# Two graph layers run group by group, or the first layer for all groups and then the second with one wide right matrix

## The chip, the core and the metric

The kernel runs on one core of a Trainium2 chip. Such a core has a matrix engine (PE; its weight loads are listed apart as PEld), a vector engine (DVE), a scalar engine (ACT), a third elementwise engine (POOL) and a queue (SP) that here does nothing but issue transfers. PE writes its sums to eight banks of PSUM, each 512 float32 wide on 128 partitions; DVE and ACT read and write PSUM and SBUF, POOL works on SBUF alone. The metric is the time of one execution on the device, in microseconds (us).

## The reference

There are 128 graphs of 128 nodes with 512 features each. Two layers follow one another, each with a residual and a layer norm.

```python
# layer 0: x (128, 128, 512), adj (128, 128, 128), W (512, 1024)
deg = sum(adj, -1)
agg = einsum('bij,bjf->bif', adj, x) / maximum(deg, 1e-6)
x = layernorm(x + relu(concat([x, agg], 2) @ W.T))

# layer 1: Wv (512, 512), Wk (3, 512, 512)
Xw = x @ Wv + bv
sj, si = Xw @ aw[:512, 0], Xw @ aw[512:, 0]
e = leaky_relu(sj[:, None, :] + si[:, :, None] + ab[0], 0.2)
alpha = adj * exp(e)
T = alpha / (sum(alpha, -1) + 1e-12)
H, Xk = 0, x
for k in range(3):
    H, Xk = H + Xk @ Wk[k] + bk[k], einsum('bij,bjd->bid', T, Xk)
x = layernorm(x + relu(H))
```

All of it is float32. Since T acts on the left and the weights on the right, H is x Wk0 + T (x Wk1 + T (x Wk2)) plus the biases. Likewise agg W' is A (x W') with A the row-scaled adjacency. So each layer is one large product of x with weights, and then small products with a 128 x 128 matrix for each graph. Both kernels work in this order. The scores sj and si are products of x with two vectors of 512.

## The kernel before

**Groups and streams.** Four graphs make a group; there are 32 groups. For each group two sequences of PE work are written out as Python generators. `stream0` (line 287) is the first layer of the group, 18 steps long (`NA`, line 671). `stream1` (line 563) is the second layer of two graphs, so it runs twice for a group. The main loop (lines 769 to 776) takes one step of the first and one step of the second in turn; the second lags 24 steps (`LAG`), so it works on the group before. Everything else, the loads, turns, sums, norms and scores, is a function that is put at a numbered half step by three tables (`EARLY`, `PLACES`, `LATE`, lines 685 to 721). Each engine carries out its instructions in exactly the order in which the Python code emits them.

**Fast products.** The large products are made by the seven-product scheme (Strassen in Winograd's form): both operands are cut into 2 x 2 blocks, sums of blocks are formed, and seven block products take the place of eight. In the first layer two levels are used: the operand is 512 rows (four graphs) by 512, the right one 512 x 512 (twice, for x and for agg), so there are 49 products of 128 x 128 by 128 x 256. `outer_pair` (line 256) makes two outer products at once, the two halves of a bank; its products are called `prod(bank, k)`. `x_turn`, `x_inner` and `x_s1` to `x_s4` (lines 214 to 233) turn x and form its left sums. In the second layer one level is used for each two graphs: seven products by [Wk2 Wk1], each of two matmuls with 512 columns, and seven by Wk0, each of two with 256 columns, with `left_sums` formed by `y_sums` (line 247). `wk_sums` (line 657) forms the right sums once.

**How one outer product runs.** The products accumulate in four banks, called X, Y, W and Z. The first product goes to X; ACT copies X to Y, a second goes to Z and ACT copies it to s5; a third is added to X, and DVE forms W = X + s5; one product is added to Y, which is then done; a further one is added to X and DVE forms Z = X + s5; one product is added to W, and the last to X. So a product into X has to wait until an addition has read X. All matmuls come from line 251, in `mm`.

**Between the layers.** `residual` (DVE) takes relu, adds x and sums the row; `y_stats`, `y_scales` and `y_norm` (ACT and POOL) make the norm. `y_scores` (line 446) takes the two dots of the unnormalized y with `wrow` on DVE, eight for a group. y is stored to memory (`y_store`) and loaded again in 32-row blocks (`y_load`), which together with a DVE transpose inside 32 x 32 blocks turns it. T takes the same road: `t_scores` stores the scores (`scd`), `t_load` loads them on all partitions, `t_exp` (ACT) makes leaky relu and exp, `t_sums` (DVE) multiplies by the adjacency and sums, `t_norm` scales, and T goes to memory (`sd`) and back (`Tb`) to be turned. The y tiles have four buffers (`py`).

Of the kernel before, what the change touches and what calls it, by code (L numbers as in the profile page):

```python
# [16 lines left out]
def kernel(  # L17
# [14 lines left out]

# [5 lines left out]
    H = NC // 2  # L61
    FH = F // 2
    G = 4
    NG = B // G
    assert N == P and F == 512 and wk.shape[2] == F and K == 3 and B % G == 0
    DEG_EPS, ROW_EPS, LN_EPS, SLOPE = 1e-6, 1e-12, 1e-5, 0.2

# [3 lines left out]
    py = ctx.enter_context(tc.tile_pool(name="py", bufs=4))  # L71
    dram = ctx.enter_context(tc.tile_pool(name="dram", bufs=3, space=bass.MemoryType.DRAM))
    small = ctx.enter_context(tc.tile_pool(name="small", bufs=4))
    psum = ctx.enter_context(tc.tile_pool(name="psum", bufs=1, space=bass.MemoryType.PSUM))


    R = 32
    Q = P // R
    xbs, adjs, ys = {}, {}, {}

    def load_blocks(dst, src):

        M = src.shape[2] // Q
        for q in range(Q):
            nc.sync.dma_start(dst[q * R : (q + 1) * R].rearrange("r b j m -> r (b j) m"),  # L85
                              src[:, :, q * M : (q + 1) * M].rearrange("b (j r) m -> r (b j) m", r=R))

    def load_x(g, p):

        b = g * G + 2 * p  # L90
        ys[g, p] = py.tile([P, 2, F], FP, name="y")
        nc.sync.dma_start(ys[g, p], x[b : b + 2].rearrange("b n f -> n b f"))

    def load_x_blocks(g, p):
        b = g * G + 2 * p
        xbs[g, p] = p2.tile([P, 2, Q, P], FP, name="xb", tag="xb")
        load_blocks(xbs[g, p], x[b : b + 2])

    def load_adj(g):
        adjs[g] = p2.tile([P, G, N], FP, name="ag")  # L100
        nc.sync.dma_start(adjs[g], adj[g * G : (g + 1) * G].rearrange("b i j -> i b j"))


    wf = const.tile([P, 7, 7, FH], FP)
    wk_sb = const.tile([P, K, NC, F], FP)
    wvt_sb = [py.tile([P, H, F], FP, name=f"wvt{i}", tag="y") for i in range(2)]
# [3 lines left out]
    bk_sb = p1.tile([K, F], FP, name="bk_sb", tag="scr")  # L110

    def load_w0(engs, o):
        src = w0t[(F if o in (0, 2) else 0) + 0 :]
        for q in range(Q):
            r0 = q * P + (o // 2) * H * R
            engs[q % len(engs)].dma_start(wf[q * R : (q + 1) * R, o, :4].rearrange("s (c n) m -> s c (n m)", c=H),
                          src[r0 : r0 + H * R].rearrange("(c s) o -> s c o", s=R))

    load_w0([nc.scalar], 0)
    load_x_blocks(0, 0)  # L120
    load_w0([nc.scalar, nc.sync], 2)
    load_x_blocks(0, 1)
# [8 lines left out]
    nhalf = const.tile([P, 2], FP)  # L131
    nc.gpsimd.memset(nhalf, -0.5)
    eps = const.tile([P, 2, G], FP)
    nc.gpsimd.memset(eps[:, 0], DEG_EPS)
    nc.gpsimd.memset(eps[:, 1], ROW_EPS)
    sj = const.tile([P, R], FP)
    nc.gpsimd.memset(sj, 0.0)
    ones = const.tile([P, 1], FP)
    nc.gpsimd.memset(ones, 1.0)
    nc.gpsimd.dma_start(bk_sb, bk)  # L140
    nc.gpsimd.dma_start(bv_sb, bv)
    nc.gpsimd.dma_start(aw_sb, aw)
    nc.gpsimd.dma_start(ab_sb, bass.AP(tensor=ab.tensor, offset=ab.offset, ap=[[0, P], [1, 1]]))

# [5 lines left out]

    wrow = const.tile([P, 2, F], FP)
    bias = const.tile([P, F], FP)
    cc = const.tile([P, 1], FP)

    def fold_constants():
# [3 lines left out]
        nc.scalar.copy(bias, pb)  # L161
        t4 = small.tile([P, NC], FP, name="t4")
        nc.vector.tensor_add(t4, aw_sb[:, 0], aw_sb[:, 1])
        nc.vector.tensor_mul(t4, t4, bv_sb)
        t1 = small.tile([P, 1], FP, name="t1")
        nc.vector.tensor_reduce(t1, t4, AX.X, ALU.add)
        yield
        nc.tensor.matmul(pc[:, :1], ones_row, t1, start=True, stop=True)
        nc.vector.tensor_sub(bias[:, FH:], bias[:, FH:], bias[:, :FH])
        nc.vector.tensor_add(cc, pc[:, :1], ab_sb)  # L170
        yield
        for c in range(NC):
            nc.tensor.matmul(pw[:2], aw_sb[:, :, c], wvt_sb[c // H][:, c % H, :], start=(c == 0), stop=(c == NC - 1))
            if c % 2:
                yield
        w2row = p1.tile([2, F], FP, name="w2row", tag="scr")
        wm = small.tile([2, 1], FP, name="wm")
        nc.scalar.activation(w2row, pw[:2], AF.Copy, accum_out=wm)
        nc.vector.tensor_scalar(wm, wm, 1.0 / F, None, ALU.mult)
        nc.vector.tensor_scalar(w2row, w2row, wm, None, ALU.subtract)  # L180
        yield
        for t in range(2):
            pr = bB[3 * t]
            nc.tensor.matmul(pr, ident[:2, t : t + 1].to_broadcast([2, P]), w2row, start=True, stop=True)
            nc.scalar.copy(wrow[:, t], pr)
            yield

    LEFT = [None, 0, 1, 6, 3, 4, 5, 2]
    RIGHT = [None, 0, 2, 3, 6, 4, 5, 1]

    def right_sums(eng, t):

        eng[0].tensor_sub(t[4], t[1], t[0])
        eng[1].tensor_sub(t[5], t[3], t[4])
        eng[2].tensor_sub(t[1], t[3], t[1])
        eng[3].tensor_sub(t[6], t[2], t[5])
# [7 lines left out]
    V, S_, L_ = nc.vector, nc.gpsimd, nc.scalar  # L207


    xu = const.tile([P, 2, 7, P], FP)  # L210
    xl = const.tile([P, 2, 7, P], FP)
    xs = const.tile([P, 2, 7, P], FP)

    def x_turn(g, p, i):
        t, src = (xu, xl)[p], xbs[g, p]
        V.transpose(t[:, :, 2 * i : 2 * i + 2].rearrange("p o k (j r) -> p j o k r", r=R),  # L216
                    src[:, i].rearrange("p j (o k s) -> p j o k s", o=2, k=2))

    def x_inner(g, p):
        t = (xu, xl)[p]  # L220
        left_sums([V, V, V, V], [t[:, :, i] for i in range(7)])

    def x_s1(g):
        V.tensor_add(xs[:, 0], xl[:, 0], xl[:, 1])

    def x_s3(g):
        S_.tensor_sub(xl[:, 0], xu[:, 0], xl[:, 0])

    def x_s2(g):
        V.tensor_sub(xs[:, 1], xs[:, 0], xu[:, 0])  # L230

    def x_s4(g):
        S_.tensor_sub(xu[:, 1], xu[:, 1], xs[:, 1])

    def left_of(i):
        return {1: xu[:, 0], 2: xu[:, 1], 3: xu[:, 1], 4: xl[:, 1], 5: xs[:, 0], 6: xs[:, 1], 7: xl[:, 0]}[i]

    def right_of(i):
        return wf[:, RIGHT[i]]

    def y_turn(g, p, i):
        if i == 0:
            yfs[g, p] = p2.tile([P, 7, H, P], FP, name="yf")
        V.transpose(yfs[g, p][:, 2 * i : 2 * i + 2].rearrange("p a h (j r) -> p j (a h) r", r=R),
                    ybs[g, p][:, i].rearrange("p j (c s) -> p j c s", s=R))

    def y_sums(g, p):
        left_sums([V, V, S_, S_], [yfs[g, p][:, i] for i in range(7)])

    def mm(dst, lhsT, rhs, start=False):  # L250
        nc.tensor.matmul(dst, lhsT, rhs, start=start, stop=True, skip_group_check=True)  # L251


    ans, aTs, ybs, yfs, scs, Ts, TTs = {}, {}, {}, {}, {}, {}, {}

    def outer_pair(i, j, evict):

        def prod(bank, k, start=False):
            for h, o in enumerate((i, j)):
                mm(bA[bank][:, h * FH : (h + 1) * FH], left_of(o)[:, LEFT[k]], right_of(o)[:, RIGHT[k]], start and h == 0)  # L260
# [245 lines left out]
    def a_load(g):  # L506
        ans[g] = swap_in("an")
# [295 lines left out]
```

## Time and profile before

| what | value |
|---|---|
| three runs | 2227.57, 2227.92, 2228.74 us (median 2227.92) |
| span of the profiled execution | 2226.0 us |
| PE busy | 2197.0 us (99%) |
| DVE, ACT, POOL busy | 1367.5 (61%), 1055.9 (47%), 679.8 us (31%) |
| moved by the DMA engines | 226.60 MB, mean 102 GB/s |
| mean granted clock of PE | 0.996 of full |

The profile is of a single execution, whose span runs from the first instruction to the last; the runs are timed from outside, so their median stands 1.9 us over it. A row of instructions gives the line, the engine, the operation, what it writes and reads, the shape and the count; after the bar come busy time in us and the mean length of one in ns; after the second bar the engine's idle time just before, and who ended it. The ends of matmuls are modelled and each overlaps the next, so the spacing of their starts, and not their mean length, is what one costs. In the tables by stage each engine has its busy time in the stretch and in brackets its instructions.

### The profile page before, as it was taken

The page shows a single profiled execution, that of the slowest core. Times are in us where ns is not written, and L with a number is a line of the kernel's source. Part 1 is how long each engine was busy: PE and PEld are TensorE (multiplying, and loading weights), DVE is VectorE, ACT ScalarE, POOL GpSimd, SP SyncE. Part 2 cuts the span into 40 slices and gives each one's busy share as a digit, 9 for nine tenths or more (in the row PEclk, how much of TensorE's full clock was granted, in tenths as well). Part 3 has the DMA queues.
Part 4 walks back from the last instruction along what each step waited for, and adds up shares of the span by engine and source line. Part 5 has one row for each costly group of instructions (what it writes and reads, how often), then busy time and mean ns, then how long its engine had stood idle before and what let it go on. Part 6 is the DMA issues. An engine that isn't in the chain of part 4 may idle for free. (4 is left out here: it accounts for less than half of the span.)

```text
span 2226.0 us, 24892 instructions
## 1 busy us (share of the span) xinstructions
PE 2197.0 (99%) x7534; PEld 1427.7 (64%) x7534; DVE 1367.5 (61%) x3206; ACT 1055.9 (47%) x2427; POOL 679.8 (31%) x977
## 2 busy tenths in 40 slices
PE   8899999999999999999999999999999999999998
PEld 5566666666666666666666666666666666666654
DVE  5766666566665566665666665666655666656652
ACT  1454544554444544444544445545445444455443
POOL 2433232232233232323322322322232323223221
PEclk9999999999999999999999999999999999999999
DMA  8343334433334433344323344333444333443321
GB/s 189 105 111 86 102 87 108 123 97 94 89 92 124 121 86 95 88 105 124 109 81 98 94 112 123 94 92 86 100 124 113 87 100 90 105 124 101 85 81 48
DMA packets 392039, 226.60 MB, mean 102 GB/s; under 512 B 155357, under 2 KB 335581, under 8 KB 391904
## 3 DMA queue, kind: packets, MB, share of 16 engines
q1 hardware_dynamic: 390656, 223.16, 37.8%
q10 hardware_dynamic: 1120, 1.84, 0.4%
q8 instruction: 59, 0.97, 0.2%
q14 instruction: 76, 0.62, 0.1%
q0 software_dynamic: 128, 0.01, 0.0%
HBM read 140.52 MB, written 84.41 MB: 101 GB/s over the span
## 5 line engine op out<-in xcount | busy, mean ns | idle before, releaser
L251 PE MATMUL bB<-wk_sb,yf 128*128 128x512 f32 (+1 forms) x2048 | 723.4, 486 | 3.5 <-DVE bB L609 1.7
L251 PE MATMUL bB<-t,yf 128*128 128x512 f32 (+1 forms) x1536 | 557.9, 486 | 1.0 <-ACT bB L576 1.0
L251 PEld LDWEIGHTS bB<-wk_sb,yf 128*128 128x128 f32 x2048 | 388.3, 190 | 238.9 <-issue 200.4
L251 PEld LDWEIGHTS bB<-t,yf 128*128 128x128 f32 x1536 | 291.8, 190 | 192.9 <-issue 161.4
L251 PE MATMUL bA<-wf,xu 128*128 128x256 f32 x1358 | 343.4, 385 | 7.0 <-DVE xu L202 4.6
L204 POOL TENSOR_TENSOR yf<-yf 128x256 f32<-128x256 f32 x64 | 57.8, 903 | 926.6 <-DVE yf L202 910.7
L251 PEld LDWEIGHTS bA<-wf,xu 128*128 128x128 f32 x1358 | 254.7, 191 | 109.5 <-issue 61.2
L251 PEld LDWEIGHTS bA<-wf,xl 128*128 128x128 f32 x924 | 176.0, 191 | 81.1 <-issue 57.2
L251 PE MATMUL bA<-wf,xl 128*128 128x256 f32 x924 | 223.0, 380 | 3.6 <-DVE xl L216 3.6
L251 PE MATMUL bA<-wf,xs 128*128 128x256 f32 x868 | 209.1, 381 | 2.0 <-DVE c L298 2.0
L251 PEld LDWEIGHTS bA<-wf,xs 128*128 128x128 f32 x868 | 165.8, 191 | 51.6 <-issue 29.2
L268 DVE TENSOR_TENSOR bA<-bA,hs 128x512 f32<-128x512 f32 x93 | 65.1, 700 | 189.2 <-PE bA L251 184.9
L450 DVE SCALAR_TENSOR_TENSOR scr<-y,wrow 128x512 bf16<-128x512 f32 x256 | 176.9, 691 | 5.6
L436 ACT ACTIVATE junk<-y,mvo 128x512 bf16<-128x512 f32 x128 | 92.4, 722 | 142.8 <-POOL mvo L435 136.9
L331 ACT COPY bA<-c 128x512 f32<-128x512 f32 x31 | 18.3, 590 | 247.9 <-DVE y L621 235.3
L463 ACT ACTIVATE y<-y,mv,sc 128x512 f32<-128x512 f32 x128 | 104.9, 822 | 62.3 <-POOL mv L457 62.3
L308 DVE TENSOR_TENSOR r<-bA,r 128x256 f32<-128x256 f32 x124 | 46.9, 420 | 136.8 <-ACT c L307 135.0
L251 PE MATMUL bB<-v,TT 128*128 128x512 f32 x256 | 130.7, 592 | 0.0
L621 DVE SCALAR_TENSOR_TENSOR y<-bB,y 128x512 f32<-128x512 f32 x128 | 88.1, 688 | 58.9 <-PE bB L251 58.8
L251 PE MATMUL bB<-u,TT 128*128 128x512 f32 x256 | 120.6, 593 | 0.6 <-DVE TT L560 0.6
L303 DVE TENSOR_TENSOR r<-bA,r 128x256 f32<-128x256 f32 x124 | 46.7, 419 | 116.9 <-ACT s L302 116.9
L583 ACT COPY u<-bB 128x512 f32<-128x512 f32 x64 | 37.5, 586 | 148.6 <-PE bB L251 148.6
(154 smaller groups left out, 2906.7 us busy)
## 6 DMA issues: line engine op xcount, KB each, us to landing
xb<-in_x_dram SPq DMA_DIRECT2D x256, 128.0 KB
y<-in_x_dram SPq DMA_DIRECT2D x64, 512.0 KB
yd<-y SPq DMA_DIRECT2D x128, 256.0 KB
yb<-yd SPq DMA_DIRECT2D x256, 128.0 KB
out_dram<-y SPq DMA_DIRECT2D x128, 256.0 KB
ag<-in_adj_dram SPq DMA_DIRECT2D x32, 256.0 KB
sd<-an SPq DMA_DIRECT2D x32, 256.0 KB
anb<-sd SPq DMA_DIRECT2D x128, 64.0 KB
```

Of the source, the lines that this page charges most:

```text
L204: eng[2].tensor_sub(t[5], t[4], t[0])
L251: nc.tensor.matmul(dst, lhsT, rhs, start=start, stop=True, skip_group_check=True)
L268: V.tensor_add(bA[2], bA[0], s5)
L303: V.tensor_add(r[:, b], bA[b][:, FH:], r[:, b])
L308: V.tensor_add(r[:, b], bA[b][:, FH:], r[:, b])
L331: L_.copy(bA[0].rearrange("p (a m) -> p a m", a=2), c22[:, 1:3])
L436: L_.activation(junk, t, AF.Square, bias=mv[:, 0:1], accum_out=mv[:, 1:2])
L450: V.scalar_tensor_tensor(scr, y, 1.0, wrow[:, t], ALU.mult, ALU.mult, accum_out=scs[g][:, t, b : b + 1])
L463: L_.activation(t, t, AF.Identity, bias=mv[:, 0:1], scale=rstd)
L583: L_.copy(u[:, 0], Y)
L621: V.scalar_tensor_tensor(r, bB[1 + i], 0.0, r, ALU.max, ALU.add, accum_out=mv[:, i, 0:1])
```

## The change

The kernel is reorganized in four ways.

1. **All groups of the first layer come first, then all groups of the second.** The normalized x of every graph is kept in memory between them (`held`), and loaded again twice: in blocks to be turned, and by rows for the residual. The adjacency is loaded again too. The y tiles have two buffers.
2. **One right matrix for the second layer.** Wk2, Wk1, Wk0 and the two score vectors stand side by side, 512 x 1538, filled up with zeros to 1540 columns. Two levels of seven products are used on it with the four graphs of a group as left operand, as in the first layer: 49 products of 128 x 128 by 128 x 385. The right sums are formed on POOL in pieces during the first layer (`w_slot`), stored and loaded over the first layer's weights at the seam (`wg_load`). The sums beta of the biases are added inside outer product 5.
3. **Two lanes of banks.** In the first layer lane 0 runs "P12" and "P56" (pairs of outer products), lane 1 "P74" and "T" (the last one, then the products with A). In the second, the outer products are called O1 to O7 and the products with T "C" (`combine`); `PA`, `PB`, `PT` (the seam) and `PL` (the last group) write out in which order their steps are taken. Small letters stand for the group before: "t.3" is step 3 of T of the group before. `PLACES_A`, `PLACES_B`, `PLACES_L` place the rest.
4. **Sums of outer products** are formed by DVE while it empties the banks (`adding`), by ACT and DVE (`copying`), and by POOL (`sum_r`, `sum_c`, and the addition to s5). The dots on DVE, the second layer's own left sums and the old bank sequence fall away. Several first-layer sums move from DVE to POOL, and for the last group T is turned by TensorE instead of through memory.

The core of the diff; the placement tables and the unchanged parts are left out:

```diff
-    def stream1(g, p):
-        lf = yfs.pop((g, p))
-        def prod(dst, k, f, start=False):
-            for c in range(H):
-                mm(dst, lf[:, LEFT[k], c], f[RIGHT[k]][:, c], start and c == 0)
-        X, Y, W, Z = bB
...
-        mm(W, tT(0), u[:, 0])
-        L_.copy(v1[:, 0], W)
-        mm(Z, tT(1), u[:, 1])
...
+    def last(lane, g):
+        a, b, c, d = lane
+        X, Z, Y, W, E = a[:, :FH], a[:, FH:], b[:, :FH], b[:, FH:], d[:, :FH]
...
+        prod(X, 6)
+        V.tensor_add(W, X, s5[:, :FH])
+        prod(Y, 2)
+        V.tensor_add(s5[:, FH:], s5[:, :FH], df[:, 2])
+        yield
+        prod(X, 7)
+        V.tensor_add(Z, X, s5[:, FH:])
+        prod(W, 3)
+        need(("sum_c22", g))
+        L_.copy(rows(c), c22[:, 0, :, :FH])
+        yield
...
+    def outer(lane, g, o, evict_y, direct, bias=False, early=None):
+        need(("wg_load", o))
+        n = NG + g
+        X, Y, W, Z = [t[:, :BW] for t in lane]
+
+        def prod(dst, k, start=False):
+            mm(dst, left_of(n, o)[:, LEFT[k]], wg[o][:, RIGHT[k]], start)
+        s5 = halves()[:, :BW]
+        if bias:
+            L_.copy(X, beta[:, 0])
+        prod(X, 1, not bias)
+        L_.copy(Y, X)
+        prod(Z, 5, True)
+        if bias:
+            V.tensor_add(s5, Z, beta[:, 1])
+        else:
+            L_.copy(s5, Z)
+        yield
+        prod(X, 6)
+        V.tensor_add(W, X, s5)
+        if early:
+            early(s5)
+        prod(Y, 2)
+        evict_y(BY, Y)
+        yield
+        prod(X, 7)
+        direct(X, s5)
+        prod(W, 3)
+        evict_y(BWW, W)
+        yield
+        prod(X, 4)
+        late.append((evict_y, BX, X))
...
+    def adding(lane, g, o, dst, src, made=None):
+        def evict(b, t):
...
+            V.tensor_add(part(dst, b, BW), t, part(src, b, BW))
...
+        def early(s5):
...
+            S_.tensor_add(s5, s5, part(src, BZ, BW))
...
+        def direct(X, s5):
+            V.tensor_add(part(dst, BZ, BW), X, s5)
+        yield from outer(lane, g, o, evict, direct, early=early)
...
+    def combine(lane, g):
...
+        def one(b):
+            mm(at_[b], TTs[g][:, b], row(b, 0, F, 0), True)
+            v = v1[b] = v1s[(g * G + b) % 3]
+            V.tensor_add(v[:, :258], at_[b][:, :258], row(b, F, 2 * BW, 0))
+            V.tensor_add(v[:, 258:], at_[b][:, 258:], row(b, 0, 254, 1))
+            L_.copy(at_[b], row(b, 254, 766, 1))
+
+        def two(b):
+            mm(at_[b], TTs[g][:, b], v1[b])
+            late.append((residual, n, b, at_[b]))
...
+    PA = "P12.1 p74.3 P12.2 p74.4 t.1 P12.3 t.2 P12.4 P56.1 t.3 t.4 P56.2 t.5 t.6 t.7 P56.3 P74.1 P56.4 P74.2".split()
+    PT = "O1.1 O1.2 p74.3 p74.4 t.1 O1.3 t.2 O1.4 t.3 t.4 O2.1 O2.2 t.5 t.6 t.7 O2.3".split()
+    PB = ("o3.4 O1.1 O2.1 O1.2 O1.3 O1.4 O2.2 O2.3 O5.1 O2.4 O5.2 "
+          "O6.1 O5.3 O6.2 O5.4 O6.3 O7.1 O6.4 O7.2 O4.1 O7.3 O4.2 "
+          "O7.4 O4.3 c.1 O4.4 O3.1 c.2 O3.2 c.3 c.4 O3.3").split()
+    PL = ("o3.4 O1.1 O2.1 O1.2 O1.3 O1.4 O2.2 O2.3 O5.1 O5.2 O2.4 O6.1 O5.3 "
+          "O6.2 O5.4 O7.1 O6.3 O7.2 O7.3 O6.4 O7.4 O3.1 c.1 c.2 c.3 O3.2 "
+          "c.4 O3.3 O4.1 O3.4 O4.2 O4.3 O4.4 x.1 x.2 x.3 x.4").split()
```

## The prediction

> **What bounds the kernel now.** I read the page's first part for the busiest engine, then the table by stage over two steady groups, then the groups of instructions with shapes kept apart, then the tail in order of time.
>
> ```profile
> PE 2197.0 (99%) x7534; PEld 1427.7 (64%) x7534; DVE 1367.5 (61%) x3206; ACT 1055.9 (47%) x2427; POOL 679.8 (31%) x977
> 1000.00:1067.72 67.72, 67.72 (x235) 44.28 (x235) 42.30 (x101) 33.01 (x76) 20.82 (x30) 1.00 0.37 102
> 1067.72:1135.44 67.72, 67.72 (x235) 44.20 (x235) 42.12 (x101) 33.09 (x76) 20.82 (x30) 1.00 0.38 102
> ```
>
> Columns of the second and third: stretch, length, busy PE, PE loads, DVE, ACT, POOL (counts), TensorE clock, DMA share, GB/s. PE has no idle time in a steady group; a group lasts 67.72 us (the score store is issued at 607.09 and again at 674.81).
>
> ```profile
> L251 PE MATMUL bB<-wk_sb,yf 128*128 128x512 f32 x1024 | 470.4, 592 | 0.0
> L251 PE MATMUL bB<-wk_sb,yf 128*128 128x256 f32 x1024 | 253.0, 380 | 3.5 <-DVE bB L609 1.7 <-ACT bB L595 1.6
> 1001.54 3.60 PE L251 MATMUL bB<-wk_sb,yf 128*128 128x512 f32 x8
> 1004.98 1.89 PE L251 MATMUL bA<-wf,xu 128*128 128x256 f32 x8
> 1006.71 1.88 PE L251 MATMUL bB<-t,yf 128*128 128x512 f32 x4
> ```
>
> Each product in the code is two PE instructions. Their means (592, 380 ns) overlap, so I take start to start: 3.44 us/8 = 430 ns for 512 columns, 1.73/8 = 216 for 256. A group has 154 of 256 and 80 of 512: 33.3 + 34.4 = 67.7, the measured group. So PE streams, at 0.833 ns a column plus 3.1 ns an instruction, and a product of 385 columns costs 2 x 324 ns (interpolated).
>
> ```profile
> 2211.90 1.03 PE L251 MATMUL bB<-t,yf 128*128 128x256 f32 x4
> 2213.03 0.43 DVE L609 TENSOR_TENSOR bB<-bB,os 128x256 f32<-128x256 f32 x1 [1.29 <-PE bB L251]
> 2213.51 1.78 PE L251 MATMUL bB<-wk_sb,yf 128*128 128x256 f32 x7 [0.58 <-DVE bB L609]
> ```
>
> Where nothing covers it, PE's last product ends at 2212.93, DVE starts 0.1 later, works 0.43, PE resumes 0.05 after. A first batch after such a wait takes 0.1 more (1.13 against 1.03 us at 2209 and 2210). These are my prices for a wait.
>
> [...]
>
> **PE's work, changed.** Second layer before: per group 56 instructions of 512 and 56 of 256 (two batches of 28 products), plus 16 of 512 for the transition. After: 7x7 products = 98 of 385, plus the same 16. First layer unchanged (98 of 256, 8 of 512).
> Per group: 98 x 0.2165 + 8 x 0.430 = 24.65; 98 x 0.324 + 16 x 0.430 = 38.62; sum 63.28 against 67.72.
> Whole program, counting built products: before 2471 of 256 and 1295 of 512 = 2183 us; after 1575 of 256, 1568 of 385, 400 of 512 = 2043.5 us. So 139 us go. Before's remaining 43 us (2226.0 - 2183) are its two ends: 29 idle[...].
>
> **The other engines.** DVE loses, per group, 6.2 us of score dots, 15.9 in all with the old second-layer additions and turns, and 2.2 of first-layer sums that go to POOL; it gains 30 additions of 385 (16.7), 8 of about 256 (3.4), turns and inner sums (7.2): +9.7, so about 52 of 63 us. In the first layer 22.5 us of durations meet 24.65 of PE. ACT gains 3.5 us (20 copies of 385 at 0.48, between its rows of 0.38 for 256 and 0.58 for 512, and 4 of 0.58, less 8.4 of old copies). POOL gains about 20, to some 41: five 385-wide additions at 1.0, four 770-wide at 1.8, four more left sums of 896 at 2.1 and the 1024-wide one taken from DVE at 2.4, less 3.3 of old inner sums; the rows of 256 (0.73), 512 (1.27), 896 (2.09) and 1024 (2.36) give these. The one-time weight sums, 36 POOL instructions, lie in POOL's gaps, at 1 to 1.8 us a slot. All of this costs nothing while PE's 63 us cover it: every engine stays under that, but each serves PE in a fixed order, so it must also be in time. Without that cover, DVE's +9.7 alone would undo PE's gain of 4.4 per group.
> DMA: x' is read twice and the adjacency twice, 1.25 MB more per group; the share rises from 0.37 to about 0.5. Issues stay near 38 a group on SP, at 0.4 to 0.5 us each. y has two buffers, not four, so a y load waits for the store before it: in layer 1 store and load have some 10 us to the residual and need about 6. Taken as hidden.
>
> **The new waits on PE.** I followed one steady group of each stage in the built order, with row durations.
> 1. "t.3" of the last outer product: X's product, DVE adds X + s5 into W, then Y's product; Y and W are halves of one bank, so PE waits for DVE (in the kernel before, Y's product stood ahead and the other layer's step behind). From the start of X's second instruction: end, start of DVE, addition, back to PE, less the 0.216 that PE streams anyway, and the restart: 0.38 + 0.07 + 0.43 + 0.05 - 0.216 + 0.1 = 0.8 us. Behind it on PE stand t.4 and the other lane's whole sequence.
> 2. "O1.2 O1.3", "O1.3 O1.4", "O2.2 O2.3" are steps of one lane in a row. X's next product may start only when DVE has read X: 0.49 + 0.07 + 0.56 + 0.05 = 1.17, of which the product between covers 0.97; plus 0.1: 0.3 each, 0.9.
> 3. After "c.4" two residuals (0.62 each) stand in DVE before O3's addition: 0.3.
> 4. O5 begins with an ACT copy of beta into X's bank, and its first product adds to that. It is queued behind the leaky relu and exp of T, which wait for T's load. Counted from the last transition product, T's scores leave 4.5 us later (O3's last product, its eviction, four small DVE steps and a turn); store 2.6 (issue to issue) and load about 3.0; T activations 1.9, copy 0.5: 12.5. PE gets there after 12.0 (0.43 of that product, 16 products of 0.648 and the four waits of points 2 and 3). I take 0.5. Bounds: 0, and 2.7 if T lands as late as now.
>
> ```profile
> 607.09 0.54 SPq L518 DMA_DIRECT2D scd<-turned  x1
> 609.72 0.39 SPq L529 DMA_DIRECT2D T<-scd  x1
> 614.90 1.28 ACT L536 ACTIVATE T<-T,si 128x128 f32<-128x128 f32 x4 [0.80 <-DMA T<-scd]
> ```
>
> Here T takes 7.8 us, of which 5.2 from its issue: y's 512 KB and two stores follow on the queue and share the engines. In the last group T is issued at 2165.93 with two stores 0.4 behind. Tenths of a microsecond from 2165.5, as the DMA view gives them:
>
> ```profile
> GB/s 0 0 0 0 0 0 0 0 0 0 0 0 0 0 123 20 143 205 164 20 143 143 184 205 184 164 246 328 307 389 369 369 328 348 348 389 451 389 328 225
> ```
>
> The first bytes move at 2166.9, one microsecond after issue, and T's 256 KB are done near 2168.5, where the stores take over. In the changed order nothing follows T on SP's queue until T itself is stored again, and the adjacency ahead of it was issued long before, so I take 3.0 with the semaphore.
> 5. Rest: ACT late for t.2's seeds (its layer norm stands ahead), x_s2 on POOL just in time for P56.1, two(3) behind a copy: 0.4 in all, between 0 and 2.
> Sum 0.8 + 0.9 + 0.3 + 0.5 + 0.4 = 2.9 us a group, x 31 = 90. Ends: 43 + 8 (last group's T by TensorE, five PE-idle us, and four norms instead of two after the last product, 3 us) + 3 at the seam where weights replace weights = 54.
> Span: 2043.5 + 54 + 90 = 2187.5, against 2226.0. The runs' median stands 1.9 over the span (2227.9), so 2189.
>
> **Rivals.** *The whole gain*: waits vanish since loads and the other lane cover them: 2043.5 + 54 + 1.9 = 2099. For it: no idle PE now. Against: the waits of 1 and 2 are in the built order, and nothing lies between. Anything under 2145 counts here.
> *T late (the slow side)*: T lands 7.8 us after the score store's issue, as now. ACT then holds beta's copy, PE waits 2.7 instead of 0.5: +2.2 x 31 = 68, 2257, slower. It decides from a landing of about 6.9 us (39 us/31 = 1.26 more than my 5.6). For it: every steady group now shows 7.8 to 8.1. Against: the traffic behind T is gone.
> *Helpers as bound*: DVE at 90% of the first layer, with ACT and POOL strictly in order, slips a microsecond more per group: +31, 2220 to 2250. For it: little slack, 0.4 us for x_s2. Against: walking DVE's list through a first-layer group I found it waiting for PE several times.
> *The change does not do what it says*: 385 columns, odd rows, cost PE like 512: 3136 x 0.106 = +332, 2520. Against: the linear law over two widths.
>
> **Chances.** My forecast 0.66 (own range 2145 to 2222), whole gain 0.11, T late 0.12, helpers 0.08, width 0.03. What a measurement of this kernel can tell from no change is about 0.2%, 4.5 us. Faster: 0.66 + 0.11 + 0.01; helpers' and T's lower edge give same 0.04; slower 0.18. Range 2145 to 2245: a tenth beyond on each side.
>
> **What would show it.** Products of 385 start 324 ns apart. PE waits for DVE W-additions at the places of 1 and 2, 0.3 to 0.8 us each. DVE near 76%, POOL near 60%, PE 94 to 95%. ACT waits for T before O5; if PE's wait there is over 1.3 us, T late holds. The stage of layer 1 should take 25.8 us a group, layer 2 40.4. I am wrong if either group is 1.5 us off, or if the ends take more than 65 us.

## The result and the profile after

The changed kernel took 2255.99 us (median of 4 runs, 2255.70 to 2257.11), the kernel before 2228.03 us on the same chip: a ratio of 1.0127, 95% interval 1.0113 to 1.0142. It is slower by 28 us, or 1.3%; 2189 us, and faster, was forecast, with a range of 2145 to 2245. The profiled execution has a span of 2255.3 us.

First the busy time of each engine, from the page of the changed kernel:

```profile
PE 2127.7 (94%) x7104; PEld 1311.8 (58%) x7104; DVE 1831.1 (81%) x3718; ACT 1153.4 (51%) x2686; POOL 1232.8 (55%) x944
```

PE's 94% is as forecast. DVE's 81% and POOL's 55% stand against a forecast of 76% and 60%. The forecast's 76% was a share of its own span of 2187.5 us, so 1663 us of DVE's work; the measured 1831 us are 168 more. By stage (columns as before: stretch, length, PE, PE loads, DVE, ACT, POOL), two first-layer groups in the middle, two at the end of the first layer, and two second-layer groups:

```profile
440.24:494.02 53.78, 50.42 (x213) 39.37 (x213) 48.50 (x95) 31.69 (x78) 37.69 (x28) 1.00 0.55 145
738.15:790.20 52.05, 50.20 (x213) 39.77 (x213) 43.34 (x96) 31.69 (x78) 34.80 (x24) 1.00 0.60 152
1253.81:1337.49 83.68, 80.71 (x230) 41.73 (x229) 66.44 (x139) 40.34 (x90) 39.85 (x32) 1.00 0.37 102
```

A late first-layer group takes 26.02 us, an earlier one more: from the starts of POOL's sum_s, the first 24 periods are 27.11 us in the mean, the last six 26.02, all together 26.89. A second-layer group takes 41.84 us, by the starts of ACT's beta copy, in nearly all of its 31 periods (41.72 in the mean, since the first two are shorter). Forecast were 25.8 and 40.4. PE's work per group (24.65 and 38.62 us) was not the part that was wrong, as the next view shows. It is the order in time around O5, in a second-layer group; the columns are start, duration, engine, line, operation, operands, count, and in brackets idle time and who ended it:

```profile
1271.03 1.46 PE L149 MATMUL bB<-big,xs 128*128 128x385 f32 x4
1271.28 2.07 POOL L276 TENSOR_TENSOR xu<-xu,xs 128x896 f32<-128x896 f32 x1 [2.67 <-PE bA L149]
1271.75 1.62 DVE L704 TENSOR_TENSOR rw<-rw,eps 128x4 f32<-128x4 f32 x1
1272.32 1.46 PE L149 MATMUL bA<-big,xs 128*128 128x385 f32 x4
1274.41 0.56 DVE L579 TENSOR_TENSOR bB<-bB,s 128x385 f32<-128x385 f32 x1
1275.02 1.56 PE L149 MATMUL bB<-big,xs 128*128 128x385 f32 x4 [1.24 <-DVE bB L579]
```

Four instructions of 385 columns take 1272.32 - 1271.03 = 1.29 us, 0.32 each: the width cost what was interpolated (324 ns). PE should go on at 1273.61; it starts O5.3 at 1275.02, 1.4 us later, since DVE makes O5.2's W only at 1274.41. DVE is late because an addition of four numbers per partition took 1.62 us. It ends at 1273.37; POOL's 128x896 subtraction x_s4 ends at 1273.35.

The same additions in the two kernels, as groups of instructions (busy us, mean ns), before:

```profile
L544 DVE TENSOR_TENSOR rs<-rs,eps 128x4 f32<-128x4 f32 x32 | 6.2, 195 | 1.1
L324 DVE TENSOR_TENSOR hs<-hs,d 128x256 f32<-128x256 f32 x31 | 13.0, 420 | 0.0
L224 DVE TENSOR_TENSOR xs<-xl 128x896 f32<-128x896 f32 x31 | 33.8, 1092 | 1.0
```

and after:

```profile
L704 DVE TENSOR_TENSOR rw<-rw,eps 128x4 f32<-128x4 f32 x32 | 47.2, 1474 | 1.1
L410 DVE TENSOR_TENSOR s<-s,d 128x256 f32<-128x256 f32 x31 | 45.4, 1466 | 0.0
L264 DVE TENSOR_TENSOR xs<-xl 128x896 f32<-128x896 f32 x63 | 118.3, 1878 | 0.0
```

The operations and sizes are the same. Additions with one operand in PSUM have not changed (256 columns, 420 ns at L308 before and 417 at L342 after; 385 columns, L607, 557 ns; the forecast's 16.7 us for 30 of them are 557 each). In the kernel before, in order of time, the small addition meets an idle POOL:

```profile
1027.37 0.80 POOL L435 TENSOR_SCALAR mvo<-mvo 128x1 f32<-128x1 f32 x2
1028.86 0.16 DVE L544 TENSOR_TENSOR rs<-rs,eps 128x4 f32<-128x4 f32 x1
1029.43 0.19 POOL L455 TENSOR_SCALAR ve<-mvo 128x2 f32<-128x2 f32 x1 [1.26 <-ACT junk L436]
```

The forecast left out that the two engines may hold each other up, and the trace looks like it: the small addition starts 0.47 us after x_s4 and ends 0.02 us after it. In 29 of the 32 groups it starts while x_s4 runs, takes 1.27 to 1.63 us and ends 0.02 us after it; in the other three no POOL instruction runs at its start, and it takes 0.16. The three rows that have grown are of additions with all inputs in SBUF. POOL was busy 31% of the time before and is busy 55% now. So far this is a reading of the trace; the experiments test it.

The rival that gave the right time, T late (2257 us), did not happen. From the view of the score tile's instructions, T's load from issue to landing, least, median, most:

```profile
DMA to landing us min/median/max: 3.0/3.2/3.4
```

The scores' store is issued 2.1 us before that load (928.3 and 930.4 in the first group), so T lands 5.3 us after it; 5.6 was assumed, 6.9 would have been needed.

### The profile page after: what moved, and what is told of

It reads as the page before. It is cut to its first block, busy times and chain, and to the rows that moved or that the text cites. A ratio compares the mean times of both kernels' runs of the same rounds, so it can differ in the third digit from the quotient of the medians.

```text
span 2255.3 us, 25848 instructions
## 1 busy us (share of the span) xinstructions
PE 2127.7 (94%) x7104; PEld 1311.8 (58%) x7104; DVE 1831.1 (81%) x3718; ACT 1153.4 (51%) x2686; POOL 1232.8 (55%) x944
## 4 chain that ended last, share of the span: by engine, by line
PE 53%; DVE 22%; ACT 8%; POOL 7%; issue 6%; DMA 3%; SPq 0%; DVEq 0%; ACTq 0%; POOLq 0%
PE bB L149 30%; PE bA L149 22%; ACT y L515 3%; DVE y L382 3%; DVE rw L704 2%; POOL s L360 2%; DVE xu L253 2%; ACT junk L502 2%; DVE bB L579 2%; POOL rstd L509 1%; POOL s L611 1%; DMA xb<-in_x_dram 1%; POOL ve L508 1%; DVE r L342 1%; DVE rw L703 1%
## 5 line engine op out<-in xcount | busy, mean ns | idle before, releaser
L149 PE MATMUL bA<-big,xu 128*128 128x256 f32 (+1 forms) x1834 | 568.0, 437 | 8.2 <-ACT bA L571 1.6
L149 PEld LDWEIGHTS bA<-big,xu 128*128 128x128 f32 x1834 | 341.6, 190 | 196.5 <-issue 31.6
L149 PE MATMUL bA<-big,xs 128*128 128x256 f32 (+1 forms) x1316 | 379.5, 420 | 2.9 <-DVE bA L313 1.6
L149 PE MATMUL bB<-big,xl 128*128 128x256 f32 (+1 forms) x1330 | 379.8, 417 | 0.1
L149 PE MATMUL bB<-big,xu 128*128 128x256 f32 (+1 forms) x868 | 287.0, 447 | 52.5 <-ACT bB L399 27.9
L149 PEld LDWEIGHTS bA<-big,xs 128*128 128x128 f32 x1316 | 244.1, 189 | 113.6 <-DVE r L614 17.3
L149 PEld LDWEIGHTS bB<-big,xl 128*128 128x128 f32 x1330 | 250.4, 190 | 89.5 <-DVE bB L313 3.2
L149 PE MATMUL bB<-c,TT 128*128 128x512 f32 x512 | 243.1, 597 | 0.0
L515 ACT ACTIVATE y<-y,mv,rstd 128x512 f32<-128x512 f32 x256 | 204.0, 811 | 48.7 <-POOL mv L510 45.3
L502 ACT ACTIVATE junk<-y,mv 128x512 bf16<-128x512 f32 x256 | 185.5, 725 | 75.4 <-POOL mv L497 72.3
L382 DVE SCALAR_TENSOR_TENSOR y<-bB,y 128x512 f32<-128x512 f32 x256 | 168.6, 685 | 20.2 <-PE bB L149 13.8
L607 DVE TENSOR_TENSOR r<-bA,r 128x385 f32<-128x385 f32 x192 | 107.0, 557 | 36.0 <-PE bA L149 31.7
```

The lines of the kernel that those rows point to most:

```text
L382: V.scalar_tensor_tensor(y, t, 0.0, y, ALU.max, ALU.add, accum_out=mvs[n][:, b, 0:1])
L502: L_.activation(junk, ys[n, b // 2][:, b % 2], AF.Square, bias=mvs[n][:, b, 0:1], accum_out=mvs[n][:, b, 1:2])
L515: L_.activation(y, y, AF.Identity, bias=mvs[n][:, b, 0:1], scale=rstds[n][:, b : b + 1])
L607: V.tensor_add(part(dst, b, BW), t, part(src, b, BW))
```

## The experiments

Theory A: in the second layer, the small addition of the row sums stands still beside POOL's x_s4, and this costs PE 1.4 us a group. Rival B: DVE simply has too much to do. Theory D: in the first layer POOL's weight subtractions, taken as free, cost 1.1 us in each of the first 24 groups. Later E and F: POOL's sums, which follow one another as a chain, or DVE's load, bind the first layer. Times are medians; 2256.0 is the changed kernel, and ratios are to the kernel before on the same chip.

### The second layer

**eps_as_constant.** The addition loses its second SBUF input.

```diff
-        V.tensor_add(rw, rw, eps[:, 1])
+        V.tensor_scalar(rw, rw, ROW_EPS, None, ALU.add)
```

> One edit in the second layer's row sums: the 128x4 addition of a stored epsilon (two SBUF inputs) becomes an addition of a constant (one SBUF input). Theory A (a DVE instruction with two SBUF inputs stands still while a POOL instruction runs): its row falls from 1.47 us to about 0.2, PE's stall at O5.3 from 1.4 us to at most 0.1, the layer-2 group from 41.84 to about 40.5 us, and the run from 2256 to about 2213 us (2205 to 2225). Rival B (DVE has too much work altogether, and it doesn't matter which instruction is the long one) would see the same, since work leaves DVE's queue; the next run parts the two. Rival C (PE waits at O5.3 for T or for the beta copy, not for DVE): no change.

2256.2 us, nothing gained. Its row:

```profile
L704 DVE TENSOR_SCALAR rw<-rw 128x4 f32<-128x4 f32 x32 | 47.3, 1479 | 1.1
```

The form with one input and a constant stands still just as long (1479 ns, and 1474 with two inputs). So the condition of two SBUF inputs, on which the edit rested, does not hold here. Whether the addition stands still beside x_s4 this run leaves open.

**sums_before_turn.** Order alone.

```diff
-        ("x_s2", 1): 38, ("t_scores", 0): 65, ("x_turn", 1, 0, 0): 14,
+        ("x_s2", 1): 38, ("t_scores", 0): 65, ("x_turn", 1, 0, 0): 16,
```

> Order alone: in the second layer one 128x512 turn of the next group's left factors (0.70 us) stands after the row sums of T and after O5.1's addition, instead of ahead of them. Every instruction is kept, and all that stood ahead of O5.2's addition into W still does. The small addition of epsilon then starts at about 0.65 us earlier in the group, some 0.1 to 0.2 us before POOL's x_s4 (2.07 us) starts. Theory A: its row falls from 1.47 us to 0.2 in most groups, O5.3's stall goes, the group is about 40.5 us, the run about 2213 us; where the small margin fails, less. Rival B (DVE's load, not the collision): no change, 2252 to 2258.

2213.96 us, 42 less, and 0.9935 [0.9920, 0.9950] of the kernel before. The group is 40.30 us. In order of time:

```profile
1261.68 0.16 DVE L704 TENSOR_TENSOR rw<-rw,eps 128x4 f32<-128x4 f32 x1
...
1261.79 2.09 POOL L276 TENSOR_TENSOR xu<-xu,xs 128x896 f32<-128x896 f32 x1 [2.67 <-PE bA L149]
```

The addition gets in 0.1 us ahead of POOL; the row's mean is 221 ns. One group of 31 misses and takes 42.35 us. No work was taken from DVE, so B falls in the second layer.

**no_pool_sum_beside.** The direct test: DVE's and PE's orders as in the changed kernel, POOL's instruction gone. The kernel leaves out a sum that O3 needs, so it serves for timing alone.

```diff
-        S_.tensor_sub(xu[n][:, 1], xu[n][:, 1], xs[n][:, 1])
+        if n < NG:
+            S_.tensor_sub(xu[n][:, 1], xu[n][:, 1], xs[n][:, 1])
```

> DVE's and PE's orders stay as in the changed kernel; only POOL's 128x896 subtraction x_s4 (2.07 us), which starts 0.5 us before the small addition of the row sums, is left out in the second layer (so the left factor of O3 is not the right one). Theory A (the small addition stands still while this POOL instruction runs): the addition's row falls from 1.47 us to about 0.2, the layer-2 group from 41.84 to 40.3 us, the run to about 2214 us, as when the addition was moved ahead of it. Rival (the place in DVE's queue, not POOL, makes it long): no change.

2213.8 us, group 40.38 us, and the addition is short again:

```profile
L705 DVE TENSOR_TENSOR rw<-rw,eps 128x4 f32<-128x4 f32 x32 | 5.2, 162 | 1.1
```

A is shown from both sides: the pair costs 42 us when it meets, and it is enough to move the one or to leave out the other.

**outer1_outer2_mixed.** This tests step 2 of the forecast, the waits inside O1 and O2.

```diff
-    PB = ("o3.4 O1.1 O2.1 O1.2 O1.3 O1.4 O2.2 O2.3 O5.1 O2.4 O5.2 "
+    PB = ("o3.4 O1.1 O1.2 O2.1 O1.3 O2.2 O1.4 O2.3 O5.1 O2.4 O5.2 "
```

> Order alone, in the second layer: O1 and O2 alternate from step to step (O1.1 O1.2 O2.1 O1.3 O2.2 O1.4 O2.3) instead of two and three steps of one lane in a row. The second step of the forecast (0.3 us at each of O1.2-O1.3, O1.3-O1.4 and O2.2-O2.3; the trace has 0.61 + 0.36) says: 0.97 us of waits go and one pair (O1.1 O1.2) of 0 to 0.3 stays, so 0.6 to 0.9 us in each of 31 groups, 19 to 28 us shorter, about 2232. But in the changed kernel as it is these waits also let DVE catch up before O5.3, where it is 1.4 us late; if all that is won comes back there (the rival), the run is under 8 us shorter.

2265.65 us, 10 more; groups of about 42.1. In order of time:

```profile
1263.20 1.56 PE L149 MATMUL bB<-big,xu 128*128 128x385 f32 x4 [0.45 <-ACT bB L571]
...
1274.16 1.20 DVE L704 TENSOR_TENSOR rw<-rw,eps 128x4 f32<-128x4 f32 x1
...
1277.02 1.56 PE L149 MATMUL bB<-big,xs 128*128 128x385 f32 x4 [1.53 <-DVE bB L579]
```

The longer waits of step 2 are gone, O1.2 now waits for ACT, and all that was won, and more, is waited for elsewhere, most of it at O5.3, where DVE still meets x_s4. The expectation's rival named the place, but put the run at a little under the changed kernel, not over it. A wait ahead of a later one on the same engine was not worth its own length here: 0.97 us a group were to be won, and 10 us of the run were lost.

### The first layer

**no_weight_sums.** The subtractions in `wg_outer` and `wg_inner` are left out, so the second layer's weight sums are not formed.

```diff
-        S_.tensor_sub(d, m, n)
+        pass
...
-        S_.tensor_sub(tmp[:, d], m, n)
+        pass
...
+    S_.memset(tmp, 0.0)
```

> The 36 subtractions that build the second layer's weight sums on POOL during the first layer are left out (a zero is stored where they stood), everything else stays. Theory D (these subtractions delay POOL's own sums and lock DVE out in the first 24 groups): the first layer's group is 26.0 us throughout instead of 27.1 on average in those, the run 24 x 1.1 = 26 us shorter, 2230 (2225 to 2235). Rival (the first 24 groups are longer for another reason, such as the weights' stores and loads on the DMA queues, which stay): under 5 us.

2231.15 us, 25 less; the period is 26.03 us in all groups but one (26.30). PE's waits there, for ACT's seeds and for DVE at t.3, fall from 27.6 and 20.2 us to 12.2 and 15.8. The DVE rows of the groups, too, come nearer to those of before:

```profile
L411 DVE TENSOR_TENSOR s<-s,d 128x256 f32<-128x256 f32 x31 | 23.4, 756 | 0.0
L543 DVE TENSOR_TENSOR deg<-deg,eps 128x4 f32<-128x4 f32 x32 | 5.2, 163 | 1.1
```

(1466 and 790 ns in the changed kernel.) D holds: the 28 subtractions of 385 columns and 8 of 770, 42 us of POOL's time, were not in gaps. How they cost PE 25 us can be read in the longest of these groups of the changed kernel, 28.94 us:

```profile
401.38 1.82 POOL L202 TENSOR_TENSOR big<-big 128x770 f32<-128x770 f32 x1
405.21 2.36 POOL L372 TENSOR_TENSOR c<-c,c 128x1024 f32<-128x1024 f32 x1
405.85 1.75 DVE L542 TENSOR_TENSOR deg<-deg,eps 128x4 f32<-128x4 f32 x1
```

The subtraction (L202) stands in the chain of POOL's sums and moves those behind it by 1.75 us, and so onto other instructions of DVE. In the same group without the subtractions the maximum L542 takes 0.16 us instead of 1.75, the addition L410 0.78 instead of 1.60, and one sum of `x_inner` 0.42 instead of 1.92. Over the first 24 groups, leaving out 1.75 us of POOL's work a group shortens DVE's instructions by 3.3 us, nearly all of it in five rows of two SBUF inputs. So the collision carries the cost here too, as far as the trace tells; POOL's own delay was not tested apart from it.

**turn_and_no_weight_sums.** Both edits (the weight sums are again not formed), against the forecast as a whole.

> Two of the edits together, the row sums ahead of the turn and no weight subtractions on POOL (a zero stands for them). If these two collisions are all that the forecast missed and they are independent: groups of 26.03 and 40.30 us, 2256 - 42 - 25 = 2189 us (2186 to 2192). If the one hides a part of the other: more.

2188.0 us (2186.2 to 2190.0), groups of 26.03 and 40.30 us. The two add up, and what is left is the time forecast, 2189. That it fits to 1 us is in part luck: the first layer's groups are 0.2 us longer than forecast, some 7 us together, and the two ends shorter by about as much.

**first_layer_one_input.** Two small DVE sums.

```diff
-        V.tensor_tensor(deg, deg, eps[:, 0], ALU.max)
+        V.tensor_scalar(deg, deg, DEG_EPS, None, ALU.max)
...
-        V.tensor_add(s5[:, FH:], s5[:, :FH], df[:, 2])
+        V.tensor_add(s5[:, FH:], E, df[:, 2])
```

> In the first layer two DVE instructions lose their second SBUF input: the sum s5 + d takes its first operand from PSUM instead of from the copy in SBUF (the same numbers), and the degree's maximum takes a constant instead of a stored epsilon. Theory A: the rows fall from 1.47 to about 0.42 us and from 0.79 to about 0.2, so DVE has 1.6 us less per group; the wait at t.3 is about 0.2 us shorter in the groups with weight sums, the run 3 to 15 us shorter. Rival B (the first layer is bound by DVE's load): 1.6 us a group, 48 us shorter. Rival (neither): no change.

2250.4 us, 6 less. The sum from PSUM takes 415 ns instead of 1466; the maximum with a constant keeps its 801. The next sum with two SBUF inputs, `x_inner`'s first, took over the standing still (601 to 992 ns), so DVE gained little, and the run is no test of B's 48 us.

**t3_spread** and **norms_after_seeds** are to take PE's waits at t.3 and t.2 away, one each.

```diff
+        prod(Y, 2)
         prod(X, 6)
         V.tensor_add(W, X, s5[:, :FH])
-        prod(Y, 2)
...
-P56.1 t.3 t.4 P56.2 t.5
+P56.1 t.3 P56.2 t.4 t.5
```

> Order alone, in the first layer's last outer product: Y's product stands ahead of X's sixth, and the other lane's step P56.2 between t.3 and t.4, so that no product directly follows an addition into its own bank or reads a bank that DVE still reads. The first step of the forecast (0.8 us a group at t.3; the trace of the changed kernel has 20.2 us of waits in 30 groups, 0.67 each, with the restart 0.77) says: the wait goes, the late first-layer groups go from 26.0 to about 25.3 us, the run is 15 to 24 us shorter, about 2236. Rival (DVE is so loaded there that PE only meets it one product later): under 6 us.

```diff
-("ln_apply", 0, 2): 78, ("ln_apply", 0, 3): 79, ("ln_apply", 0, 0): 81, ("ln_apply", 0, 1): 84,
-("y_store", 0, 1): 87, ("y_store", 0, 0): 89, ("load_y", 0, 1): 51, ("load_y", 0, 0): 52,
+("ln_apply", 0, 2): 85, ("ln_apply", 0, 3): 87, ("ln_apply", 0, 0): 89, ("ln_apply", 0, 1): 91,
+("y_store", 0, 1): 89, ("y_store", 0, 0): 92, ("load_y", 0, 1): 53, ("load_y", 0, 0): 55,
```

> Order alone, on ACT in the first layer: the four normalising activations of the group before (0.81 us each) stand behind the two copies that seed t.1's and t.2's banks, three of them no longer ahead; y's stores and loads move 2 to 4 half steps later with them. If ACT's order is what makes t.2 late (27.6 us of waits in 29 groups): the wait goes from 0.95 us a group to under 0.1, also in the groups with weight sums, and the run is 20 to 30 us shorter, about 2231. Rival (the seeds wait for POOL's sums, not for ACT): the wait stays at over 0.6 us in the groups with weight sums and the run is at most 10 us shorter. If y's later stores and loads collide with the residual, the gain is given back and the waits name y's load.

Both were slower. t3_spread: 2357.9 us, late groups of 27.8 to 29.5. The wait at t.3 went, but t.4's addition L413 now stood in DVE's queue behind P56.2's and behind `x_inner`:

```profile
882.90 0.40 DVE L241 TENSOR_TENSOR xl<-xl 128x256 f32<-128x256 f32 x1
...
884.48 0.42 DVE L413 TENSOR_TENSOR bB<-bB,s 128x256 f32<-128x256 f32 x1
...
884.96 0.70 PE L149 MATMUL bB<-big,xu 128*128 128x256 f32 x2 [2.30 <-DVE bB L413]
```

In the early groups this wait reaches 4.3 us, and the granted clock falls as well: 0.977 in the mean of the run, against 0.995 to 0.997 in the runs of the kernel before. It is this edit's fault, then, and no verdict on the step. norms_after_seeds: 2279.8 us. The 27.6 us at the seeds (ACT's copies into the banks, to which t.2's products add) went to nothing, and PE waited 57.7 us in four other places, of which 20.2 at t.3 were there before (us in total, times, longest):

```profile
PE bB L149 <- DVE bB L408: 25.7, 29, 1.5
PE bB L149 <- DVE bB L413: 13.1, 17, 0.8
PE bA L149 <- POOL xs L268: 10.4, 23, 1.2
PE bA L149 <- DVE bA L318: 8.5, 12, 2.3
```

DVE also waited 12.4 us, up to 3.3 at once, for y's loads: two y buffers bear the order of the changed kernel, but not stores that come 2 to 4 half steps later. **five_orders**, these and the second-layer orders together, took 2357.1 us.

> Together: the row sums ahead of the turn, the first layer's sum from PSUM, t.3 spread, the norms after the seeds, O1 and O2 mixed. If the waits are independent, 2256 - 42 - 6 - 20 - 25 - 23 = 2140, faster than the kernel before (2228). If the first layer's DVE (90% busy) binds as soon as its waits are gone, the first layer keeps about 1 us a group and it is 2170. The PE stream of 2043 and ends of some 45 us put the floor at 2090.

Its first layer is about as slow as that of t3_spread (29.7 us a group in the mean, 30.3 there), and its second has groups of 42.2 us although the sums stand ahead of the turn: the mixed order shifts PE, and the addition (1276.10) again starts 0.5 us after x_s4 (1275.60); its row is 1297 ns. So the cure by order hangs on a few tenths of a microsecond.

**first_layer_reordered.** A second, more careful order, on top of sums_before_turn: t.3 with Y's product first and P56.1 behind it, the degree's steps (and ACT's `a_norm` that uses them) later, the sum from PSUM, one normalising activation fewer ahead of the seeds.

```diff
-P12.4 P56.1 t.3 t.4 P56.2
+P12.4 t.3 P56.1 t.4 P56.2
...
-("degree", 0): 12, ("a_norm", 0): 18,
-("ln_apply", 0, 3): 79, ("ln_apply", 0, 0): 81, ("ln_apply", 0, 1): 84,
+("degree", 0): 20, ("a_norm", 0): 22,
+("ln_apply", 0, 3): 85, ("ln_apply", 0, 0): 86, ("ln_apply", 0, 1): 88,
```

> Order, with the row sums ahead of the turn in the second layer; in the first layer t.3 with Y's product first and between P12.4 and P56.1, the degree's three small steps on DVE behind t.4's addition, the sum s5 + d from PSUM, and two instead of three normalising activations ahead of the seeds on ACT, with y's stores where they were. Against the row sums' move alone (2214): if the waits at t.2 and t.3 (0.4 and 0.5 us in the late groups, 0.9 and 0.7 in the early) are what DVE's and ACT's order makes, 0.6 to 1.2 us less in 30 groups, 2178 to 2196; if DVE and POOL bind the first layer whatever the order, as the run with the norms after the seeds suggests, 2210 to 2225.

2209.6 us, only 4 less than 2214. The waits at t.2 and t.3 are gone, and 27.5 us are waited for at the transition (the products with A) instead:

```profile
755.06 0.59 ACT L416 COPY bB<-c 128x512 f32<-128x512 f32 x1 [0.47 <-POOL c L376]
...
757.33 1.28 ACT L549 ACTIVATE an<-ag,rdeg 128x128 f32<-128x128 f32 x4 [0.31 <-DVE rdeg L544]
...
759.14 2.85 PE L149 MATMUL bB<-c,TT 128*128 128x512 f32 x6 [1.30 <-ACT bB L419]
```

POOL's c22 (L376) holds ACT's first copy, and `a_norm`, put there by this edit, stands ahead of the second (L419). The order itself gave nothing to the groups: the early ones take 26.94 us, as with the sum from PSUM alone (first_layer_one_input), and the late ones 26.18 instead of 26.02.

**first_layer_and_weight_slots** and **weight_slots_stores_apart** put the weight subtractions into POOL's idle stretch between residuals; `ln_mean_half` scales the first two means ahead of them. The second run gives each store a place of its own (the last line of the edit).

```diff
-("w_slot", 0, 0): 0, ("w_slot", 0, 1): 16,
+("ln_mean_half", 0): 65, ("w_slot", 0, 0): 27, ("w_slot", 0, 1): 28,
...
+("w_slot", 0, 2): 10,
```

> The kernel of the run before with POOL's weight subtractions moved into its idle stretch between the second and the fourth residual of a group (the mean's scaling is split in two so that POOL gets there in time), one in a group, two where both are of 385 columns. If they collide with nothing there, what leaving them out gave comes in full: 20 to 25 us less than the run before. If they only collide with other sums of DVE's (the left factors' inner sums follow within a microsecond): under 10 us less.

> The reordered first layer with the weight subtractions in POOL's idle stretch, as in the run at 2208, but each store of a weight sum gets a place of its own 11 us before the next subtraction, since there two groups of 30.9 and 30.7 us waited on POOL for such a store. Those 9 us go and nothing else changes: 2198 to 2202 us. If other waits take their place: 2206 to 2210.

2208.4 and 2200.75 us. In the first, most groups were shorter but two took 30.9 and 30.7 us, waiting for a store. In the second the first 24 periods are 26.52 us in the mean (26.94 without the edit). At 0.9876 [0.9859, 0.9892] of the kernel before it is the fastest that computes the whole reference.

**scales_behind_chain, scales_and_weight_slots, scales_alone, third_y_buffer.** What binds the first layer once PE's waits are moved? E: POOL's sums in a row, from r to c22.

```diff
-("ln_scales", 0): 76, ("ln_apply", 0, 2): 78, ("ln_apply", 0, 3): 79, ("ln_apply", 0, 0): 81, ("ln_apply", 0, 1): 84,
+("ln_scales", 0): 87, ("ln_apply", 0, 2): 88, ("ln_apply", 0, 3): 89, ("ln_apply", 0, 0): 90, ("ln_apply", 0, 1): 92,
...
+    p3 = ctx.enter_context(tc.tile_pool(name="p3", bufs=3))
```

> The first layer reordered as before, plus: the layer norm's three small POOL steps (ln_scales, about 2.2 us with their standing still) go from between sum_s and sum_d to behind sum_c22, the normalising activations and y's stores after them, and y has three buffers instead of two so that its loads need not wait for that. Theory E (with PE's waits at t.2 and t.3 gone, the first layer is bound by POOL's chain from the last sum of r to c22: sum_s 2.4, ln_scales 2.2, sum_d 1.7, x_s2 2.1, sum_c21 2.4, sum_c22 2.4, together 13.1 us, that ends in ACT's copies of c22 and PE's wait for them, 1.3 to 1.5 us at the transition): the chain is 2.2 us shorter, that wait goes, the late groups are 24.8 to 25.3 us and the early ones about 1 us shorter, the run 2165 to 2190. Rival F (DVE's load binds it): the late groups stay at 25.8 us or more, the run over 2200.

> The same, with the weight subtractions in POOL's idle stretch between the residuals. Theory E: they no longer stand in the chain; 2155 to 2185 us, the early groups as long as the late ones but for a few. Rival F: over 2195.

> The row sums ahead of the turn, ln_scales behind sum_c22 with three y buffers, but t.3 and the rest of the first layer in the order of the changed kernel. Against 2214 us: theory E: the wait at t.2 (0.4 to 0.9 us, ACT behind POOL's ln_scales) goes and the transition doesn't wait instead, since the chain is shorter: 10 to 30 us less, with t.3's 0.7 us left. Rival F: within 5 us.

> The control for the third buffer of y alone, added to the reordered first layer (2210 us): theory E and rival F both say no change (within 3 us), since no wait for y's load shows there; more than that, and the buffer carries part of the other runs' gain.

2435.1, 2439.3 and 2416.2 us, against 2210.1 for the third buffer alone (no change). The three tell nothing on E or F, since moving the scales made ACT's queue stand still, here in scales_behind_chain:

```profile
837.42 1.52 ACT L516 ACTIVATE y<-y,mv,rstd 128x512 f32<-128x512 f32 x2 [5.43 <-POOL mv L511]
...
841.01 2.07 PE L150 MATMUL bB<-big,xu 128*128 128x256 f32 x4 [5.99 <-DVE bB L410]
```

ACT reaches the first activation, which now waits for the end of POOL's chain, and the copies of banks behind it wait too; through them DVE's L410, and through that PE. The group is 34 us, some 8 more than before: 6 are this wait, and some 2.4 a slower PE behind it: one group earlier, after a wait of 5.70 us, twelve instructions of 256 columns take 4.99 us (806.73 to 811.72) instead of 2.6. The granted clock is 0.953 in the mean of the run, against 0.995 to 0.997 in the runs of the kernel before.

**no_scales_in_chain.** The same question without moving ACT: `first_layer_reordered` without the three POOL steps.

```diff
+        if n < NG:
+            rstds[n] = plain
+            return
```

> The reordered first layer (2210 us), but the layer norm of the first layer leaves out its three POOL steps (the rows are only centred, not scaled), so ACT's normalising activations keep their place and wait only for the mean. Theory E (POOL's chain from r's last sum to c22 binds the first layer): the chain is 2.2 us shorter, PE's wait for ACT's copy of c22 (27.5 us in 29 groups, 0.95 each) goes but for 0.1 us, the late groups fall from 26.18 to 24.7 to 25.3 us, the run to about 2175 (2165 to 2185). Rival F (DVE's load binds it): the groups stay at 25.8 us or more and the run over 2200.

2182.25 us, 27 less than with them, inside E's range; the early groups fall from 26.94 to 25.96 us, the late from 26.18 to only 25.74, between E's forecast and F's. The wait at the transition, which E said would go, stayed (30.6 us):

```profile
758.32 0.60 ACT L418 COPY bB<-c 128x512 f32<-128x512 f32 x1
...
760.75 1.28 ACT L554 ACTIVATE an<-ag,rdeg 128x128 f32<-128x128 f32 x4
761.93 0.58 ACT L421 COPY bB<-c 128x512 f32<-128x512 f32 x1
```

ACT's first copy of c22 no longer waits for POOL, the second still stands behind `a_norm`. So in the reordered kernel the three steps in POOL's chain cost 1 us of an early and 0.4 us of a late group, but not on the road that E named. What went is a wait of PE for DVE (L318, 8.5 us in 28 groups), and DVE's busy time in the early groups fell from 24.5 to 22.7 us: with the steps gone POOL's sums come earlier and DVE's meet them less. Whether the chain's own length or these collisions bind the first layer is not parted by this run, and a kernel with `a_norm` elsewhere was not tried.

## Why the prediction was wrong, point by point

**The step that failed** is "The other engines" with its sentence "All of this costs nothing while PE's 63 us cover it". It took DVE's durations from the rows of a kernel in which POOL was busy 31%, and gave POOL some 20 us more a group without asking whether its instructions lengthen DVE's. "So it must also be in time" was the right question; the answer used the row durations of before, 0.195 us for the row sums' addition, which took 1.47. That alone is the second layer's 31 x 1.44 = 45 us, of which each of the two edits that part the pair gave back 42. Within the same step "The one-time weight sums, 36 POOL instructions, lie in POOL's gaps" failed: 25 us. (The step's terms for DVE, 16.7 + 3.4 + 7.2 less 15.9 and 2.2, give +9.2 and not +9.7; nothing hangs on it.)

**The sum.** Second layer: 41.84 instead of 40.4, +45. First layer: 26.89 instead of 25.8 in the mean, times 31, +34, of which 25 are the weight sums. Ends: 2255.3 - 2043.5 - 31 x (26.89 - 24.65) - 31 x (41.84 - 38.62) = 42.5 us instead of 54, -11. Together +68, the 2255.3 - 2187.5 that was missed.

**What held.** The PE stream: 385 columns at 324 ns. Step 1, the same-bank addition at t.3: 0.79 us in a late group, 0.8 forecast. Step 2: 0.61 + 0.36 for 0.9. Step 3: 0.34 for 0.3. Step 4: the place was right and T's landing too (3.2 us for 3.0), the wait was 0.1 us in the steady group instead of 0.5. Step 5, ACT late for t.2's seeds: 0.56 us in a late group and 0.9 to 1.4 in the earlier ones looked at, of 0.4 for all the rest together. With x_s4's collision and the weight subtractions gone, the kernel takes 2188.0 us. The last group's T does leave PE idle for 5.1 us, as said; but the start is better, in the first 60 us PE is busy for 53.4 us instead of 48.1.

**The rivals.** Helpers as bound was nearest, with the right engines and a slip of about a microsecond in each layer, 1.1 and 1.4 us against 25.8 and 40.4; but it was placed in the first layer alone and given 31 us, where 79 came. T late hit the time by chance. The whole gain and the width (385 columns at the price of 512) did not come.

## What to carry to other kernels

A duration is a price only beside the neighbours it was measured with: when work goes from DVE to POOL, every DVE addition or maximum that takes all its inputs from SBUF is to be priced once more, at its own length plus up to that of the POOL instruction it can meet (here 0.42 us became up to 2.62 beside one of 2.36), and small instructions ahead of a critical addition come first. Before a wait is taken away, look at what the waiting engine does next: here the edits that removed a named wait in the first layer, or in O1 and O2, got back less than its length, or lost, since the next collision or the next queue took it. "It lies in the gaps" needs the gaps' times, not an engine's free share.

## What the runs showed of the hardware

- In the changed kernel, beside a POOL instruction of 128x896 or 128x1024 (2.1 to 2.4 us), DVE's additions of two SBUF tensors stood still: 128x4 took up to 1.63 us instead of 0.16 (a maximum up to 1.75), 128x256 up to 2.62 (1.47 in the mean of one row) instead of 0.42, and 128x896 up to 2.61 instead of about 1.09. An addition (eps_as_constant) and a maximum (first_layer_one_input) of one SBUF tensor with a constant did too (1479 and 801 ns in the mean), which the expectation had put at 0.2 us.
- Not affected beside the same POOL instructions: additions with a PSUM operand (395 to 428 ns in the mean for 256 columns), a reduction of 128x512 (0.68 us), 32 x 32 turns of 128x512 (0.67 to 0.70), a reciprocal of 128x4 (0.18).
- It goes both ways: POOL's 128x4 step L508 took 0.92 us behind DVE's 128x896 addition in the first layer and 0.19 in the second.
- Behind long waits of PE its instructions took about twice their time for some 5 us: in the changed kernel's last group, after 3.54 us and two shorter waits, six of 512 columns took 4.87 us instead of 2.6, at a granted clock of 0.53 (2229.92 to 2234.79 us); in scales_behind_chain, after 5.70 us, twelve of 256 took 4.99 us instead of 2.6. Behind 2.30 us in t3_spread (884.96) eight of 512 started 0.43 us apart, as elsewhere, and behind the changed kernel's 1.24 us at O5.3 the clock stayed full (1.00 from 1275.02 to 1276.42 us).
